# Two cross-attention layers on one core: layer 1's token-wise exponentials turned and laid over the keys, in place of a second set of scores

## The chip, the cores and the metric

The kernel runs on one core of a Trainium2 chip. The metric is the device time of one execution in microseconds (us). The kernel before was timed three times: 987.32 us median, 983.13 to 987.98. A separate execution was recorded by the hardware profiler; all views below are of that one.

The engines are named as the profile names them: PE (TensorE's matrix multiplications), PEld (its loads of the stationary operand), DVE (VectorE), ACT (ScalarE), POOL (GpSimd), SP (SyncE, which issues nearly all transfers). All data are float32. The profile shows each float32 matmul as two records.

## What is computed

Two cross-attention layers, one after the other, over the same 128 context tokens. The batch is 2, the sequence 2048, the width 512, and there are 16 heads. Layer 0 has heads of 64 and a mask; layer 1 has heads of 32, no mask and no biases in its projections. Both end with a residual and a LayerNorm.

```python
def _L1_xattn_ref(query, key, value, Wq, Wk, Wv, Wo, bo, ln_gamma, ln_beta):
    q = _split_heads(query @ Wq.T)                       # (b, 16, 2048, 32)
    k = _split_heads(key @ Wk.T)                         # (b, 16, 128, 32)
    v = _split_heads(value @ Wv.T)
    logits = scaling * jnp.einsum('bhqd,bhkd->bhqk', q, k)
    attn = jax.nn.softmax(logits, axis=-1)
    ctx = jnp.einsum('bhqk,bhkd->bhqd', attn, v)
    ctx = ctx.transpose(0, 2, 1, 3).reshape(query.shape[0], q.shape[2], H)
    projected = ctx @ Wo.T + bo
    resid = query + projected
    ...                                                  # LayerNorm over the width
x = _L0_xattn_ref(x, ctx_1024, ctx_1024, mask, ...)
x = _L1_xattn_ref(x, ctx_1024, ctx_1024, ...)
```

## The kernel before

The 4096 tokens are cut into 8 tiles t of 512. Layer 0's queries, scores, exponentials and values come first, for all tiles (some 373 us). Then a software pipeline runs in rounds: in round t, layer 1's attention of tile t, the output projection and LayerNorm of layer 0 and the query projection of layer 1 for tile n = t + 1, fetches for tile f = t + 2, and the output projection of layer 1 for tile l = t - 1. The order in each round is a list written by hand in `steps(t)`: each entry is a function's letter, its tile and its part. All five engines execute their own instructions in exactly that order; a wait in one engine's stream holds everything behind it on that engine, SP's transfers included. There are five such lists: t = -1, t = 0, the general one, the round before the last tile (n == NB - 1), and the last tile's.

Layer 1's attention works on a tile t and a group g of four heads (r = 0..3), so 4 groups per tile, 28 (tile, group) pairs without the last tile. The steps are:

- `maxima` (X), L866. For each of the four blocks i of 128 tokens and each head r, the scores with tokens on the partitions: the queries are the stationary operand, the keys stream (L873). Two PSUM tiles of two banks each hold them. DVE takes each token's maximum over the 128 keys into `tops` (L879 for heads 2 and 3, L893 for heads 0 and 1). ACT takes the exponentials of heads 2 and 3, eight instructions with the negative maximum as bias (L889). DVE subtracts the maxima of heads 0 and 1 (L894), and ACT takes one exponential over them (L897). The exponentials e serve only for their sums.
- `sums1` (U), L900: DVE sums e over the keys (L903).
- `shares1` (G), L909: reciprocals of the sums, into `tops` beside the maxima.
- `turn_maxima` (M), L913: PE turns `tops`, DVE copies it out (L918), and SP writes the rows to DRAM (L924) and reads them back spread over all partitions: the maxima over the 128 key partitions, 1 MB per group, into `p1` (L927), and the reciprocals over the 32 rows of each head, `r1` (L936).
- `scores1` (S), L941: the scores a second time, now with keys on the partitions (L948). DVE subtracts them and the maxima in `p1` (L967). In the last tile the maxima are subtracted by a matmul with `sel` (L955) and ACT takes the exponential straight from PSUM (L965).
- `exponentials1` (P1), L970: ACT, one exponential over 128 x 2048 (L972).
- `attend1` (V), L974: the values times the exponentials (L996), then DVE multiplies by the reciprocals into `ctx` (`scale1`, L1009).

`project1` (E, L1026) then projects `ctx`, `rest1` (Y, L1033) adds the residual, `moments1` (I), `norm1` (O) and `store` (W) finish the tile. Of layer 0 the rounds hold `load_residual` (F), `fetch_r` (A), `fetch_u` (L), `normalise` (N, POOL, L182), `residual` (R, POOL, L191), `project0` (Pr, L671), `rest0` (J, L678), `moments0` (K0), `norm0` (Z). The queries of layer 1 come from `turn_whole` (TW), `sums_of_turned` (TS) and seven block products `product1` and `add1` (PQ, AQ, L822), or from `turn` and `queries1` (T, Q) in the first two tiles.

PSUM is split into two score tiles with one buffer each (used by X, S and TW), two banks `mm` and two banks `av`.

Of the kernel before, what the change touches and what calls it, by code (L numbers as in the profile page):

```python
# [24 lines left out]
def two_cross_attentions(  # L25
# [81 lines left out]
    sel = const.tile([P, NG, K], F32, tag="sel", name="sel")  # L107
    for g in range(NG):
        for r in range(4):
            rows = slice(32 * r, 32 * (r + 1))  # L110
            nc.vector.tensor_scalar(
                sel[rows, g, :], ident[rows, 32 * r + g : 32 * r + g + 1].to_broadcast([32, K]),
                -1.0, None, ALU.mult,
            )
# [33 lines left out]
    rows_dram = [dram.tile([2 * NG, 4, TB], F32, tag=f"rows_{t}", name=f"rows_{t}") for t in range(NB)]  # L148
# [660 lines left out]
    def product1(t, n):  # L809
# [17 lines left out]
        if n == 1:  # L827
            q1s[t] = two.tile([P, NG, TB], F32, tag="q1", name=f"q1_{t}")
            for m in range(2):
                nc.scalar.activation(  # L830
                    q1s[t][:, m, LO], ps[:, m, :], AF.Identity, bias=bq1[:, 2 + m : 3 + m]
                )
# [21 lines left out]
    def queries1(t, g, half):  # L854
        if g == 0 and half == 0:
            q1s[t] = two.tile([P, NG, TB], F32, tag="q1", name=f"q1_{t}")
# [8 lines left out]

    def maxima(t, g):  # L866
# [3 lines left out]
        for i in range(NQ):  # L870
            for r in range(4):
                rows = slice(32 * r, 32 * (r + 1))
                nc.tensor.matmul(  # L873
                    ps[r // 2][:, r % 2, i, :], q1s[t][rows, g, i * P : (i + 1) * P],
                    k1[rows, g, b * K : (b + 1) * K], start=True, stop=True,
                )
        to = tops.rearrange("p i (r n) -> p r i n", n=32)[:, :, :, g : g + 1]
        to = to.rearrange("p r i o -> p r (i o)")
        nc.vector.tensor_reduce(to[:, 2:], ps[1], AX.X, ALU.max)  # L879
        if t == NB - 1:  # L880
            nc.vector.tensor_reduce(to[:, :2], ps[0], AX.X, ALU.max)
            return

        e = fours.tile([P, 4, NQ, K], F32, tag="p1", name=f"e_{t}_{g}")
        less = three.tile([P, 2, NQ], F32, tag="less", name=f"less_{t}_{g}")
        nc.vector.tensor_scalar_mul(less, to[:, 2:, :], -scaling)  # L886
        for r in range(2, 4):
            for i in range(NQ):
                nc.scalar.activation(  # L889
                    e[:, r, i, :], ps[1][:, r - 2, i, :], AF.Exp, bias=less[:, r - 2, i : i + 1],  # L890
                    scale=scaling,
                )
        nc.vector.tensor_reduce(to[:, :2], ps[0], AX.X, ALU.max)  # L893
        nc.vector.tensor_tensor(  # L894
            e[:, :2], ps[0], to[:, :2, :].unsqueeze(3).to_broadcast([P, 2, NQ, K]), ALU.subtract
        )
        nc.scalar.activation(e[:, :2], e[:, :2], AF.Exp, scale=scaling)  # L897
        open_x[t, g] = e

    def sums1(t, g):  # L900

        to = sums.rearrange("p i r n -> p r i n")[:, :, :, g : g + 1]
        nc.vector.tensor_reduce(  # L903
            to.rearrange("p r i o -> p r (i o)"), open_x.pop((t, g)), AX.X, ALU.add
        )

    tTs, probs1, open_x = {}, {}, {}

    def shares1(t):  # L909
        share = tops.rearrange("p i (r n) -> p i r n", n=32)[:, :, :, NG : 2 * NG]  # L910
        nc.vector.reciprocal(share, sums)

    def turn_maxima(t):  # L913
# [4 lines left out]
        nc.vector.tensor_copy(tT, tr)  # L918
# [4 lines left out]
        for r in range(4):  # L923
            nc.sync.dma_start(rows_dram[t][:, r, :], tT[32 * r : 32 * r + 2 * NG, :])  # L924
        for g in range(NG):
            p1 = fours.tile([P, 2, 2, TB], F32, tag="p1", name=f"p1_{t}_{g}").rearrange("p a b q -> p (a b) q")
            nc.sync.dma_start(p1, rows_dram[t][g].unsqueeze(0).to_broadcast([P, 4, TB]))  # L927
            probs1[t, g] = p1
            if g == NG - 2:
                fetch_r1(t, 0)  # L930
        for g in range(1, NG):
            fetch_r1(t, g)

    def fetch_r1(t, g):
        r = three.tile([P, TB], F32, tag="r1", bufs=4, name=f"r1_{t}_{g}")
        nc.sync.dma_start(r, rows_dram[t][NG + g].unsqueeze(1).to_broadcast([4, 32, TB]))  # L936
        dens1[t, g] = r
# [3 lines left out]
    def scores1(t, g):  # L941

        b, _ = where(t)
        last = t == NB - 1
        ps = sc_tiles(f"s1_{t}_{g}", [2, TB])
        for r in range(4):
# [3 lines left out]
                start=True, stop=not last,  # L950
# [277 lines left out]
```

## Time and profile before

| what | value |
|---|---|
| time of the runs, median (lowest to highest) | 987.32 us (983.13 to 987.98) |
| profiled execution, first to last instruction | 977.3 us; granted PE clock 0.997 |
| layer 0's attention (20 to 373 us) | PE busy 352.2 of 353.0 us, DVE 267.5 |
| start of the rounds (373 to 434) | PE busy 60.4 of 61.0 |
| a second steady round (738.82 to 808.70, 69.88 us) | PE busy 69.88, DVE 59.41, ACT 29.91, POOL 40.20, DMA share 0.45 |
| last tile (878 to 960) | PE busy 80.0 of 82.0 |
| after it (960 to 977.3) | PE busy 7.8 of 17.3 |

The profiled execution's record runs from its first to its last instruction; of its own time outside of that there is no record, and the median of the runs lies 10.0 us above its span. Busy time is the union of an engine's instructions in a window. Matmuls are pipelined and one record of 512 columns spans about 0.6 us while the next one starts 0.44 us after it, so durations of single records add up to more than the time they take; the distance from start to start is the better measure. The idle time of an engine that is not the bound costs nothing.

### The profile page before, as it was taken

Reading aid. Unit: us, or ns where it says so; the run is one execution under the profiler, and the core shown is the slowest. Engines: PE = TensorE matmul, PEld = TensorE weight load, DVE = VectorE, ACT = ScalarE, POOL = GpSimd, SP = SyncE. Lnnn points to the kernel's source line nnn. Section 1 sums busy time; section 2 is a strip of 40 time slices with the busy share of each in tenths; the row PEclk is TensorE's granted clock in tenths of the full one; section 3 lists DMA queues with packets and bytes.
Section 4 is the critical chain, followed back from the end, with each engine's and each line's share of the span. In section 5 each row is a group of like instructions: output and inputs, shape, how many; then the busy total and the mean of one; then the engine's idle time right before and its main releaser. Section 6 shows DMA issues by size and latency. Waiting matters only on the chain.

```text
span 977.3 us, 12755 instructions
## 1 busy us (share of the span) xinstructions
PE 958.0 (98%) x4628; PEld 448.4 (46%) x4628; DVE 731.8 (75%) x1093; ACT 414.9 (42%) x637; POOL 483.3 (49%) x403
## 2 busy tenths in 40 slices
PE   8999999999999999999999999999999999999996
PEld 4444333333333334474544644645545545545442
DVE  2577777878878872249469869879789689698867
ACT  1145345545534644044534434434344444344351
POOL 1044454543453546685453934925835736546153
PEclk9999999999999999999999999999999999999998
DMA  9314265225223436534632542632723724403311
GB/s 337 126 49 141 55 175 155 56 57 182 60 79 86 120 104 201 181 128 157 243 128 87 188 160 87 238 110 89 263 82 119 251 90 155 167 1 151 111 44 43
DMA packets 51325, 128.46 MB, mean 131 GB/s; under 512 B 9440, under 2 KB 13280, under 8 KB 47680
## 3 DMA queue, kind: packets, MB, share of 16 engines
q1 hardware_dynamic: 49536, 125.03, 38.5%
q0 software_dynamic: 1152, 2.10, 0.9%
q8 instruction: 36, 0.59, 0.3%
q10 hardware_dynamic: 576, 0.53, 0.2%
q14 instruction: 25, 0.20, 0.1%
HBM read 101.46 MB, written 26.18 MB: 131 GB/s over the span
## 4 chain that ended last, share of the span: by engine, by line
PE 76%; DVE 4%; POOL 2%; issue 1%; ACT 0%; POOLq 0%; DVEq 0%; ACTq 0%
PE pso L671 22%; PE ps L347 12%; PE pso L1026 10%; PE psq L822 8%; PE psu L491 5%; PE st L396 4%; PE s L948 3%; PE mx L873 3%; PE u L996 3%; PE psq L860 1%; PE tr L727 1%; PE den L470 1%; PE den L484 1%; DVE sums L903 1%; PE psk L591 1%
## 5 line engine op out<-in xcount | busy, mean ns | idle before, releaser
L435 POOL TENSOR_TENSOR sm<-sm,mask 128x1024 f32<-128x1024 f32 x64 | 150.4, 2372 | 202.4 <-ACT sm L434 191.4
L671 PE MATMUL pso<-wo,uT 128*128 128x512 f32 x512 | 229.2, 599 | 0.2 <-POOL uT L182 0.2
L671 PEld LDWEIGHTS pso<-wo,uT 128*128 128x128 f32 x512 | 94.5, 190 | 117.2 <-issue 109.1
L658 POOL TENSOR_TENSOR rstd<-rstd,mhalf 128x1 f32<-128x1 f32 x64 | 35.2, 550 | 213.8 <-DVE shift L662 213.7
L434 ACT ACTIVATE sm<-sm,ncs 128x1024 f32<-128x1024 f32 x64 | 70.0, 1141 | 107.6 <-DVE ncs L431 107.5
L1026 PE MATMUL pso<-wq,ctx 128*128 128x512 f32 x256 | 115.5, 600 | 0.0
L889 ACT ACTIVATE e<-mx,less 128x128 f32<-128x128 f32 x224 | 60.9, 383 | 83.6 <-DVE less L886 83.6
L972 ACT ACTIVATE p<-p 128x2048 f32<-128x2048 f32 x28 | 53.5, 1911 | 97.2 <-DVE p L967 79.5
L409 DVE CUSTOM_DVE_ANT_1 sm<-st,mask 128x1024 f32<-128x1024 f32 x64 | 75.6, 1217 | 20.9 <-DMA mask<-in_maskT_dram 13.5
L967 DVE TENSOR_TENSOR p<-s,p 128x1024 f32<-128x1024 f32 x56 | 65.8, 1217 | 29.2 <-PE s L948 28.6
L347 PE MATMUL ps<-xt,wq 128*128 128x512 f32 x180 | 83.4, 599 | 0.0
L359 DVE TENSOR_TENSOR q<-ps,q 128x512 f32<-128x512 f32 x75 | 51.9, 692 | 39.5 <-PE ps L347 35.3
L182 POOL TENSOR_TENSOR uT<-uT,r 128x1024 f32<-128x1024 f32 x32 | 75.3, 2362 | 3.7 <-issue 1.7
L1026 PEld LDWEIGHTS pso<-wq,ctx 128*128 128x128 f32 x256 | 46.5, 190 | 57.4 <-issue 48.6
L462 DVE TENSOR_TENSOR fold<-fold,sm 64x2048 f32<-64x2048 f32 x22 | 64.5, 2930 | 2.6 <-ACT fold L456 1.9
L903 DVE TENSOR_REDUCE sums<-e 128x16 f32<-128x2048 f32 x28 | 63.8, 2278 | 1.1 <-ACT e L897 1.1
L396 PE MATMUL st<-q,k 64*128 64x512 f32 x256 | 63.6, 615 | 0.0
L491 PE MATMUL psu<-sm,v 128*32 128x512 f32 x512 | 62.1, 598 | 0.8 <-ACT dens L441 0.7
L347 PE MATMUL ps<-t,s 128*128 128x512 f32 x120 | 56.4, 592 | 0.0
L347 PEld LDWEIGHTS ps<-xt,wq 128*128 128x128 f32 x180 | 33.2, 190 | 46.5 <-issue 46.4
L686 ACT ACTIVATE z<-z,shift,rstd 128x512 f32<-128x512 f32 x32 | 26.0, 814 | 66.9 <-POOL shift L663 66.9
L688 POOL TENSOR_TENSOR y<-z,g 128x512 f32<-128x512 f32 x32 | 40.6, 1269 | 23.1 <-ACT z L686 23.1
(154 smaller groups left out, 1511.0 us busy)
## 6 DMA issues: line engine op xcount, KB each, us to landing
p<-rows SPq DMA_DIRECT2D x28, 1024.0 KB
u<-u SPq DMA_DIRECT2D x32, 512.0 KB
uT<-u SPq DMA_DIRECT2D x32, 512.0 KB
xt<-in_xT_dram SPq DMA_DIRECT2D x16, 512.0 KB
z<-in_x_dram SPq DMA_DIRECT2D x32, 256.0 KB
r<-r SPq DMA_DIRECT2D x32, 256.0 KB
out_dram<-y SPq DMA_DIRECT2D x32, 256.0 KB
r<-rows SPq DMA_DIRECT2D x28, 256.0 KB
```

The source lines that it names most:

```text
L182: nc.gpsimd.tensor_tensor(u, u, r.unsqueeze(1).to_broadcast([P, 2, TB]), ALU.mult)
L347: nc.tensor.matmul(ps, w[:, c, :], x[c] if isinstance(x, tuple) else x[:, c, :], start=(c == 0), stop=(c == 1),)
L396: nc.tensor.matmul(st[n][:, j, :], k0[rows, 2 * g + n, b * K : (b + 1) * K], q[rows, :], start=True, stop=True,)
L409: nc.vector.tensor_tensor_reduce(out=sm, in0=st[n], in1=masks[t].unsqueeze(1).to_broadcast([P, 2, TB]), scale=1.0, scalar=-3.4028234e38, o ...
L434: nc.scalar.activation(s, s, AF.Exp, bias=ncs[:, i + n : i + n + 1])
L435: nc.gpsimd.tensor_tensor(s, s, masks[t].unsqueeze(1).to_broadcast([P, 2, TB]), ALU.mult)
L491: nc.tensor.matmul(ps[32 * j : 32 * (j + 1), :], v0[:, b, d : d + 32], p[j], start=True, stop=True,)
L671: nc.tensor.matmul(ps, uTs[t, n // 2][:, n % 2, i * P : (i + 1) * P], wo0s[n // 2][:, n % 2, :], start=(n == 0), stop=(n == NE - 1),)
L822: nc.tensor.matmul(ps[:, m, :], w[:, c, m * P : (m + 1) * P], y[:, c, :], start=(c == 0), stop=(c == 1),)
L903: nc.vector.tensor_reduce(to.rearrange("p r i o -> p r (i o)"), open_x.pop((t, g)), AX.X, ALU.add)
L967: nc.vector.tensor_tensor(p1[:, at], ps[n], p1[:, at], ALU.subtract)
L1026: nc.tensor.matmul(ps, ctxs[t][g][:, i * P : (i + 1) * P], wo1s[:, g, :], start=(g == 0), stop=(g == NG - 1),)
```

## The change

For tiles 0 to 6 the second scores go. The exponentials that `maxima` computes anyway, with tokens on the partitions, are laid out so that they can be turned:

- The four token blocks of `maxima` take every fourth token (`by_fours`): block i holds the tokens 4m + i. So the stationary operand steps by four elements.
- e gets its own tiles (two buffers), ordered as key block, head and token block, key within the block. ACT's eight exponentials also give the sums of their rows (`accum_out`); the maxima go to a small tile `top`, no longer to `tops`.
- `sums1` sums the remaining two heads, then DVE turns e in place in 32x32 blocks (L911 of the new kernel), and SP lays the 4 x 4 blocks over the key partitions with 16 transfers from SBUF to SBUF into `p1` (L915).
- `scores1` stays for the last tile only; its maxima are subtracted through a broadcast column of a negative identity, `minus`, in place of `sel`. `exponentials1` is gone. The broadcast of the maxima through DRAM is gone; that of the reciprocals stays.
- `attend1` reads `p1` in four pieces per head, and `scale1` writes every fourth token of `ctx`, which puts the tokens back in order.
- The queries `q1` have one buffer in place of two. The descriptor scratch of POOL's transfers is set to 2048 bytes.
- All lists of `steps` are written anew; the values of a tile now stand in the next tile's round (in the same round for t = 6).

```diff
     def maxima(t, g):
...
-                    ps[r // 2][:, r % 2, i, :], q1s[t][rows, g, i * P : (i + 1) * P],
+                    ps[r // 2][:, r % 2, i, :], by_fours(q1s[t][rows, g, :])[:, i],
...
+        e = two.tile([P, 4, 4 * NQ, 32], F32, tag="e", name=f"e_{t}_{g}")
+        nc.vector.tensor_reduce(top[:, 1], ps[1], AX.X, ALU.max)
+        nc.vector.tensor_scalar_mul(less, top[:, 1], -scaling)
         for r in range(2, 4):
             for i in range(NQ):
                 nc.scalar.activation(
-                    e[:, r, i, :], ps[1][:, r - 2, i, :], AF.Exp, bias=less[:, r - 2, i : i + 1],
-                    scale=scaling,
+                    e[:, :, r * NQ + i, :], ps[1][:, r - 2, i, :].rearrange("p (k q) -> p k q", q=32),
+                    AF.Exp, bias=less[:, r - 2, i : i + 1], scale=scaling,
+                    accum_out=sums[:, r, i, g : g + 1],
                 )
...
     def sums1(t, g):
 
-        to = sums.rearrange("p i r n -> p r i n")[:, :, :, g : g + 1]
+        e = open_x.pop((t, g))
         nc.vector.tensor_reduce(
-            to.rearrange("p r i o -> p r (i o)"), open_x.pop((t, g)), AX.X, ALU.add
+            sums[:, :2, :, g : g + 1].rearrange("p r i o -> p (r i o)"),
+            e[:, :, : 2 * NQ, :].rearrange("p k m q -> p m k q"), AX.XY, ALU.add,
         )
+        flat = e.rearrange("p k m q -> p (k m q)")
+        nc.vector.transpose(flat, flat)
+        p1 = fours.tile([P, 4, 4, P], F32, tag="p1", name=f"p1_{t}_{g}")
+        for k in range(4):
+            for a in range(4):
+                nc.sync.dma_start(
+                    p1[32 * k : 32 * (k + 1), a].rearrange("p r q -> p (r q)"),
+                    e[32 * a : 32 * (a + 1), k].rearrange("p m q -> p (m q)"),
+                )
+        probs1[t, g] = p1
...
-            p1 = fours.tile([P, 2, 2, TB], F32, tag="p1", name=f"p1_{t}_{g}").rearrange("p a b q -> p (a b) q")
-            nc.sync.dma_start(p1, rows_dram[t][g].unsqueeze(0).to_broadcast([P, 4, TB]))
...
     def scores1(t, g):
...
-                nc.vector.tensor_tensor(p1[:, at], ps[n], p1[:, at], ALU.subtract)
...
-    def exponentials1(t, g):
-        p1 = probs1[t, g]
-        nc.scalar.activation(p1, p1, AF.Exp, scale=scaling)
...
     def scale1(t, g):
-        nc.vector.tensor_tensor(ctxs[t][g], open_u.pop((t, g)), dens1.pop((t, g)), ALU.mult)
+        u, r = (v.rearrange("p (a i q) -> p a i q", a=4, q=32) for v in (open_u.pop((t, g)), dens1.pop((t, g))))
+        nc.vector.tensor_tensor(ctxs[t][g].rearrange("p (a q i) -> p a i q", a=4, i=NQ), u, r, ALU.mult)
...
+        return [
+            (F, f, 0), (R, n, 3), (X, t, 0), (J, n, 0), (A, f, 0), (F, f, 1), (A, f, 1), (V, l, 0), (F, f, 2),
+            (Pr, n, 1, 0), (A, f, 2), (K0, n, 0), (Pr, n, 1, 1), (U, t, 0), (X, t, 1), (Z, n, 0), (A, f, 3),
+            (J, n, 1), (V, l, 1), (K0, n, 1), (Pr, n, 2, 0), (U, t, 1), (Pr, n, 2, 1),
+            *([(R, n, 2)] if t > 1 else []), (X, t, 2), (J, n, 2), (V, l, 2), (K0, n, 2), (Z, n, 1),
+            (Pr, n, 3, 0), (Pr, n, 3, 1), (U, t, 2), (J, n, 3), (L, f, 0), (V, l, 3), (L, f, 1), (X, t, 3),
+            (K0, n, 3), (L, f, 2), (Z, n, 2), (L, f, 3), (F, f, 3), (E, l, 0), (Y, l, 0), (E, l, 1),
+            (Z, n, 3), (U, t, 3), (N, f, 0), (G, t), (N, f, 1), (E, l, 2), (Y, l, 1), (I, l, 1), (I, l, 0),
+            (Y, l, 2), (TW, n), (I, l, 2), (E, l, 3), (TS, n, 0), (N, f, 3), (TS, n, 1), (O, l, 0), (O, l, 1),
+            (N, f, 2), (Y, l, 3), (R, f, 0), (I, l, 3), (M, t), (PQ, n, 2), (PQ, n, 1), (PQ, n, 6), (O, l, 3),
+            (PQ, n, 7), (AQ, n, 6), (PQ, n, 5), (AQ, n, 7), (R, f, 1), (PQ, n, 4), (AQ, n, 2), (PQ, n, 3),
+            (O, l, 2), (AQ, n, 5), (AQ, n, 4), (W, l, 0), (AQ, n, 3), (W, l, 1), (W, l, 2), (Pr, f, 0, 0),
+            (Pr, f, 0, 1), (W, l, 3),
+        ]
...
-    nc = bacc.Bacc("TRN2", target_bir_lowering=False, num_devices=1)
+    nc = bacc.Bacc("TRN2", target_bir_lowering=False, num_devices=1, dynamic_dma_scratch_size=2048)
```

## The prediction, written before the changed kernel was run

> **What bounds the kernel now.** I read the page's busy times first, then the busy time of each engine stage by stage, then one steady round (one 512-token tile) in order of time.
>
> ```profile
> span 977.3 us, 12755 instructions
> PE 958.0 (98%) x4628; PEld 448.4 (46%) x4628; DVE 731.8 (75%) x1093; ACT 414.9 (42%) x637; POOL 483.3 (49%) x403
> ...
> 434.00:505.00 71.00, 68.13 (x389) 35.56 (x386) 46.38 (x58) 31.73 (x68) 38.67 (x35) 1.00 0.56 193
> ...
> 599.05:668.94 69.89, 69.89 (x365) 36.08 (x365) 59.41 (x92) 29.91 (x55) 40.18 (x40) 1.00 0.45 153
> 668.94:738.82 69.88, 69.88 (x366) 36.09 (x365) 59.41 (x92) 29.91 (x55) 40.21 (x40) 1.00 0.44 152
> ```
>
> The columns of the last rows are window, length, busy PE, PEld, DVE, ACT, POOL, then granted clock (1.00). In a steady round PE is busy for the whole 69.88 us. The kernel is as long as its PE work, so only PE work that goes, or PE waits that come, move the time. The second engine is DVE, at 59.4 us of 69.9, and it is not evenly spread:
>
> ```profile
> 597.88 1.17 PE L873 MATMUL mx<-k,q 32*128 32x128 f32 x32
> 598.98 10.73 PE L1026 MATMUL pso<-wq,ctx 128*128 128x512 f32 x24
> ...
> 618.71 1.14 PE L948 MATMUL s<-q,k 32*128 32x512 f32 x8
> 619.78 1.99 PE L822 MATMUL psq<-ts,ws 128*128 128x256 f32 x8
> ...
> 630.22 1.07 PE L996 MATMUL u<-p,v 128*32 128x512 f32 x8
> 631.22 1.99 PE L822 MATMUL psq<-yT,ws 128*128 128x256 f32 x8
> ```
>
> Start to start, maxima of a head group take 1.10 us of PE, second scores 1.07, values 1.00. A full step of layer 0's projection (L671, 16 records) runs 590.81 to 597.88, 7.07.
>
> ```profile
> L967 DVE TENSOR_TENSOR p<-s,p 128x1024 f32<-128x1024 f32 x56 | 65.8, 1217 | 29.2 <-PE s L948 28.6
> L903 DVE TENSOR_REDUCE sums<-e 128x16 f32<-128x2048 f32 x28 | 63.8, 2278 | 1.1 <-ACT e L897 1.1
> L996 PEld LDWEIGHTS u<-p,v 128*32 128x32 f32 x256 | 5.7, 108 | 24.2 <-ACT p L972 10.6 <-issue 9.4 <-ACT y L1041 3.8
> L873 PEld LDWEIGHTS mx<-k,q 32*128 32x128 f32 x1024 | 31.5, 186 | 25.2 <-issue 24.4 <-DVE p L967 0.8
> ```
>
> **Removed.** PE: four matmuls (eight records) for each of 28 (tile, group) pairs, 28 x 1.07 = 30.0 us, 4.28 per round; all of it is on the bound. DVE: 56 subtractions of 1.217 = 68.2 us. ACT: 28 exponentials (L972) of 1.911 = 53.5 us. The 28 row broadcasts of 1 MB go too. The last tile keeps its second scores, so its 4 pairs gain nothing; its `sel` weights become a broadcast of `minus`, 16 matmuls with as many columns, price nothing within 0.1 us each.
>
> **Added on ACT.** 224 exponentials get a sum; the one accumulator row that exists (L785) has a read of 0.19 us behind each ACTIVATE. Eight per group: 1.5 us, so the eight exponentials take 2.18 + 1.5 = 3.7 us. ACT has 40 us free per round, and the next user of those PSUM banks comes 9 us later; without that cover it would be 1.5 us for each of 28 pairs, 43 us.
>
> **Added on DVE.** The sum covers half the elements: 2.278 becomes about 1.14, saving 1.14. Then one 32x32 block transpose of 128x2048 in place, not in this trace. Nearest rows: the reduce over the same 2048 elements, 2.278; lower end, half of it, 1.14; upper end, twice, 4.56 (one pass to fill, one to drain). I take 2.28, equal shape and count. The division after the values (L1009, 0.69) writes every fourth element: between 0.69 and, doubled, 1.37; I take 0.69. DVE per round: 59.4 - 9.7 - 4.6 + 9.1 = 54.2, still less than PE's.
>
> But the work is not where it was. The first three quarters of a round are maxima of a group, layer 0's projection of a block, and DVE's share of both. Before: DVE 1.22 + 0.45 + 1.21 + 1.22 (maxima, L879 to L894), 0.68 (L678), 1.07 (statistics), 2.28 (sums) = 8.13, against PE 1.10 + 7.07 = 8.17: level. After, the values of the tile before are put into each quarter: PE 9.17; DVE 8.13 + 1.14 + 0.69 = 9.96. DVE falls behind by 0.79 per quarter. DVE's clock from the round's start: 1.2 + 3 x 9.96 = 31.1; the fourth block's residual and division 1.37, last maxima 4.1, statistics 1.07, first output residual (L1033) 0.68: 38.3. PE: 3 x 9.17 + 1.00 + 1.10 + two output projections of 3.54 = 36.7, and the third needs the bank that this residual empties. PE waits 1.6. Later DVE has less to do (no subtractions) and catches up.
>
> **Moved.** Second use of the queries is gone, so one buffer suffices; only the maxima read it. Values of tile t move into round t+1, their wait on exponentials (L996 above: 10.6 us of weight loads) goes; what they wait for now are transfers a round older.
>
> **Added on SP.** Sixteen transfers of 64 KB per pair, 448 in all, for 28 removed. An issue of a small transfer has a row:
>
> ```profile
> 612.04 1.30 SPq L924 DMA_DIRECT2D rows<-tT  x4
> ```
>
> 0.32 each, 5.2 us per pair, 20.8 per round. Range: 0.29 (the shortest group, L924's median) to 1.37 (uT, 5.47 us for 4, 512 KB each). I take 0.32. In the changed program's order each transfer also waits for the eighth before it in the queue; SP's waits show 2.3 us at most for a rows transfer to land, less than eight issues of 0.32. Behind the transposes' wait stand, in the queue, uT fetches (issued by my clock near 37, wanted by POOL at 42), stores, loads of the next residuals. Cover: tile `e` of a group is written again two groups later. Sums of group 0 end at 11.2; group 2's subtraction starts near 24; 12.8 us for 5.2 + 2.3. Were it late, that subtraction would hold all of DVE behind it, and the exponentials all of ACT, and PE would wait at the next maxima. [...]
>
> POOL's descriptor scratch shrinks; it serves the 8 mask loads (L234, 4.7 us in all). Between nothing and twice that, all in layer 0 where PE is busy 352.2 of 353 us; I take nothing.
>
> **Added on the weight loads.** The maxima's stationary operand is every fourth token, a step of 16 bytes; all weight loads in the trace are dense. 128 columns take 186 ns (L873), 32 take 108 (L996): 78 ns for 96 columns, 104 for 128. Lower end: nothing. Upper end: column time doubles and all shows: 32 records on four row strips, eight per strip, 8 x 0.104 = 0.83 us per group, 32 groups = 26.6 us. I take nothing: the load group's busy 0.98 of 1.10 us is overlapped, and the rows give no reason for a penalty. [...]
>
> **Sum.** A steady round: 69.88 - 4.28 + 1.6 = 67.2, a gain of 2.7; five of them, 13.5. Round t=0 (434 to 505): DVE has no division there and lags 1.1 per quarter less than its free time; 4.28 less about 0.8 for the fourth block, 3.5. Round t=6: 2.7. Last tile: nothing. Together 19.7. 977.3 - 19.7 = 957.6 for the span. The runs' median 987.32 lies 10.0 above the span; I keep that: 967.6, so **968**. Own range: without any wait 30.0 + 1.3 (waits in 434 to 505 on exponentials) gives 956; some quarters' division at 1.37 (lag +0.68 per quarter, 2 us per round, 14 in all) gives 981.
>
> **Rivals.** (a) Strided weight loads cost their upper end. A quarter of PE is then 10.0, level with DVE, and the 1.6 us wait vanishes: 69.88 - 4.28 + 3.3 = 68.9, gain 1.0 in five rounds and in t=6, 2.3 in t=0, minus 3.3 for the last tile's maxima: 5 in all, **982**. For: maxima are the group with the most weight columns per streamed column, so a slow load shows there first. Against: the loads are busy 31.5 us of the maxima's 37.6, which leaves room for part of it only if they overlap.
> (b) DVE becomes the bound of the first half of a round (the slower side). Place: the transposes behind the sums. The round is back at 69.88 when the wait grows by 2.7, that is 0.9 per quarter: from 3.2 us per transpose. At 4.56: three quarters each 2.28 later, 6.8 more, round 74.0, 4.1 over seven rounds = 29: **1016**. For: DVE was level already. Against: 2048 elements of float32 cost 2.28 in the reduce.
> (c) SP's queue becomes the bound. From (12.8 - 2.3) / 16 = 0.65 us per transfer, `e` is late. At 1.0 us a group takes 16 us against quarters of 9.96; groups 2 and 3 wait 5.5 and 6 us, 11 per round, less the 2.7: 8 over seven rounds: **1045**. For: transfers of 512 KB cost 1.37. Against: 0.32 for 16 KB.
>
> **How the numbers follow.** Within 0.5% (4.9 us) counts as no change: 982.4 to 992.3; a measurement of this kernel can't tell less, its three runs spread by 4.8. Forecast 0.47, wholly faster. (a) 0.25, half each side of 982.4: 0.12 faster, 0.13 same. (b) 0.17 and (c) 0.11, slower. Faster 0.59, same 0.13, slower 0.28. The range takes 950 (a few us below no wait at all, for covered waits that the trace hides) to 1005, which takes in (a) and the milder half of (b): some 0.15 lie above, 0.05 below.
>
> **What would show it.** Right: 28 fewer score groups, PE busy near 928; steady rounds near 67 with an idle of 1 to 2 us before the third output projection, released by DVE; transpose rows near 2.28. (a): maxima near 1.9 us start to start. (b): transposes above 3.2, maxima waiting for DVE. (c): transfers above 0.65 us, and subtractions or exponentials of the maxima released by a transfer. Wrong altogether if rounds wait where I saw cover: on uT at layer 0's projection or on p at the values.

## The result, and the profile after

The changed kernel takes 1044.99 us (median of 4 runs, 1043.72 to 1045.28) against 985.94 us for the kernel before on the same chip: a ratio of 1.0604 (95% interval 1.0581 to 1.0627). It is slower by 59 us, where 968 us and a range of 950 to 1005 had been predicted. The page of the profiled execution, and its steady rounds (window, length, busy PE, PEld, DVE, ACT, POOL, granted clock, DMA share, GB/s):

```profile
span 1042.8 us, 13088 instructions
...
PE 973.6 (93%) x4404; PEld 481.6 (46%) x4404; DVE 702.7 (67%) x1050; ACT 377.5 (36%) x833; POOL 484.1 (46%) x403
...
611.17:682.96 71.79, 68.94 (x334) 38.93 (x333) 54.83 (x87) 24.40 (x82) 38.33 (x40) 1.00 0.50 145
682.96:757.86 74.90, 70.97 (x334) 39.96 (x333) 55.60 (x87) 24.39 (x82) 41.75 (x42) 0.98 0.49 143
757.86:832.04 74.18, 70.92 (x333) 40.03 (x332) 54.65 (x87) 24.40 (x82) 40.04 (x41) 0.98 0.48 142
```

Two things are to be seen. The 224 PE records (8 x 28) of the second scores are gone, but PE is busy for 973.6 us and not for 928. And PE, busy for 98% of the span before, is now busy for 93%: it waits. A round takes 71.8 to 74.9 us where it took 69.9. The groups of instructions that answer to those shown before (line, engine, operation, count; busy us, mean ns of one; idle before):

```profile
L870 PEld LDWEIGHTS mx<-k,q 32*128 32x128 f32 x1024 | 62.7, 322 | 25.9 <-issue 24.4
L870 PE MATMUL mx<-k,q 32*128 32x128 f32 x1024 | 68.8, 405 | 0.7 <-DVE tops L878 0.7
L911 DVE STREAM_TRANSPOSE e<-e 128x2048 f32<-128x2048 f32 x28 | 64.7, 2312 | 1.0
L906 DVE TENSOR_REDUCE sums<-e 128x8 f32<-128x1024 f32 x28 | 34.0, 1215 | 6.8 <-ACT e L900 6.6
L1006 DVE TENSOR_TENSOR ctx<-u,r 128x512 f32<-128x512 f32 x28 | 31.0, 1108 | 6.7 <-DMA r<-rows 4.6 <-PE u L992 2.0
```

A weight load of the maxima went from 186 to 322 ns, and their matmuls' busy time from 37.6 (the prediction's (a)) to 68.8 us: this alone eats the 30.0 us that were removed. It leaves some 14 of the 45 us by which PE's busy time misses 928; where they come from is seen with the flat transfer below. DVE's new work has about the sizes that were forecast: 2.31 us for a transpose, 1.215 for the half sum; the division is 1.108, between the two ends given (0.69 was taken). Now a steady round in order of time, PE first, then two lines of SP's own queue, one from before this round and one from within it:

```profile
682.96 2.15 PE L870 MATMUL mx<-k,q 32*128 32x128 f32 x32
685.03 1.06 PE L992 MATMUL u<-p,v 128*32 128x512 f32 x8
...
742.09 3.68 PE L816 MATMUL psq<-yT,wq 128*128 128x256 f32 x8 [3.74 <-ACT q L824]
```

```profile
659.00 12.91 SPq L915 DMA_DIRECT2D p<-e  x16
...
696.29 11.11 SPq L915 DMA_DIRECT2D p<-e  x16
```

Start to start the maxima of a group take 2.07 us here (1.10 before). The sixteen transfers of one pair occupy SP for 11 to 13 us, 0.7 to 0.8 us each, while the DMA engines are only half busy (DMA share 0.49 above): it looks as if the issuing were full, not the bytes, which is tested below. A quarter of a round is some 10 us, and SP's queue then runs from 696.29 to 745.18 us without a gap of more than 0.2 us. How that reaches PE is clearest in round t = 0, where SP's queue reads:

```profile
476.21 12.25 SPq L915 DMA_DIRECT2D p<-e  x16
488.57 0.52 SPq L181 DMA_DIRECT2D z<-in_x_dram  x1
...
490.95 14.33 SPq L915 DMA_DIRECT2D p<-e  x16
505.32 0.58 SPq L171 DMA_DIRECT2D r<-r  x1
506.00 1.36 SPq L166 DMA_DIRECT2D uT<-u  x3
507.47 15.43 SPq L915 DMA_DIRECT2D p<-e  x16
522.99 0.53 SPq L166 DMA_DIRECT2D uT<-u  x1
523.57 0.57 SPq L171 DMA_DIRECT2D r<-r  x1
```

and PE in the same stretch:

```profile
515.20 1.99 PE L665 MATMUL pso<-wo,uT 128*128 128x512 f32 x4 [3.71 <-POOL uT L176]
518.12 1.98 PE L665 MATMUL pso<-wo,uT 128*128 128x512 f32 x4 [0.93 <-POOL uT L176]
532.36 3.78 PE L665 MATMUL pso<-wo,uT 128*128 128x512 f32 x4 [8.74 <-POOL uT L176]
```

The fourth fetch of `uT` and of `r` for layer 0's projection stands behind sixteen transfers that have nothing to do with it. They go out at 523, land some 6 us later, POOL's normalisation takes 2.35 us, and PE, which had nothing else in its order, starts at 532.36. In steady rounds the path is longer, but seems to have the same start. SP issues the fetches of `uT` from 729.69 us on, POOL's multiplications of `uT` start at 733.54 after 3.60 us of idle time, ACT's whitening then waits 9.44 us for POOL, ACT's copies of the queries come behind it, and PE waits 3.74 us at `psq`. Five rounds have such a wait, of 2.9 to 3.7 us. That POOL waits for the fetches there is inferred; with the flat transfer below POOL waits for `uT` once in the whole run (13.0 us), its idle time before these multiplications is 16.8 us in all in place of 49.1, and PE's wait for ACT at this `psq` (16.2 us in all) is gone. In the waits of ACT, the exponentials of the maxima stand behind the transfers, since `e` is not free:

```profile
ACT e L887 <- DMA p<-e: 81.9, 12, 10.9
```

(us in total, times, longest.) And the shares by line of the chain that ended last, where PE had 76% in all before and has 26% now:

```profile
SPq L915 11%; PE pso L665 8%; DMA r<-r 8%; PE pso L1023 4%; DMA uT<-u 4%; PE mx L870 3%; PE psq L854 3%; PE psq L816 2%; POOL uT L176 2%; POOL y L1041 1%; PE u L992 1%; PE ps L341 1%; POOL y L1044 1%; DMA out_dram<-y 1%; DMA p<-e 1%
```

So there are two suspects, the step of 16 bytes in the weight loads and the number of issues on SP, and a third that can't be excluded from the traces: the new order of the lists.

### The profile page after: what moved, and what is told of

Same layout as the page of the kernel before. It is cut to its first block, busy times and chain, and to the rows that moved or that the text cites. A ratio compares the mean times of both kernels' runs of the same rounds, so it can differ in the third digit from the quotient of the medians.

```text
span 1042.8 us, 13088 instructions
## 1 busy us (share of the span) xinstructions
PE 973.6 (93%) x4404; PEld 481.6 (46%) x4404; DVE 702.7 (67%) x1050; ACT 377.5 (36%) x833; POOL 484.1 (46%) x403
## 4 chain that ended last, share of the span: by engine, by line
PE 26%; DMA 17%; SPq 13%; POOL 6%; DVE 3%; issue 3%; ACT 2%; POOLq 0%; ACTq 0%; DVEq 0%
SPq L915 11%; PE pso L665 8%; DMA r<-r 8%; PE pso L1023 4%; DMA uT<-u 4%; PE mx L870 3%; PE psq L854 3%; PE psq L816 2%; POOL uT L176 2%; POOL y L1041 1%; PE u L992 1%; PE ps L341 1%; POOL y L1044 1%; DMA out_dram<-y 1%; DMA p<-e 1%
## 5 line engine op out<-in xcount | busy, mean ns | idle before, releaser
L665 PE MATMUL pso<-wo,uT 128*128 128x512 f32 x512 | 230.1, 602 | 15.3 <-POOL uT L176 15.3
L887 ACT ACTIVATE e<-mx,less 128x128 f32<-128x128 f32 x224 | 78.8, 378 | 197.1 <-DMA p<-e 81.9
L176 POOL TENSOR_TENSOR uT<-uT,r 128x1024 f32<-128x1024 f32 x32 | 75.1, 2354 | 49.1 <-DMA uT<-u 18.1
L883 DVE TENSOR_REDUCE top<-mx 128x8 f32<-128x1024 f32 x28 | 34.0, 1214 | 76.1 <-PE mx L870 76.1
L1038 ACT ACTIVATE y<-y,shift,rstd 128x512 f32<-128x512 f32 x30 | 23.3, 811 | 144.2 <-POOL shift L657 144.2
L870 PEld LDWEIGHTS mx<-k,q 32*128 32x128 f32 x1024 | 62.7, 322 | 25.9 <-issue 24.4
L870 PE MATMUL mx<-k,q 32*128 32x128 f32 x1024 | 68.8, 405 | 0.7 <-DVE tops L878 0.7
L911 DVE STREAM_TRANSPOSE e<-e 128x2048 f32<-128x2048 f32 x28 | 64.7, 2312 | 1.0
```

The lines of the kernel that those rows point to most:

```text
L176: nc.gpsimd.tensor_tensor(u, u, r.unsqueeze(1).to_broadcast([P, 2, TB]), ALU.mult)
L665: nc.tensor.matmul(ps, uTs[t, n // 2][:, n % 2, i * P : (i + 1) * P], wo0s[n // 2][:, n % 2, :], start=(n == 0), stop=(n == NE - 1),)
L870: nc.tensor.matmul(ps[r // 2][:, r % 2, i, :], by_fours(q1s[t][rows, g, :])[:, i], k1[rows, g, b * K : (b + 1) * K], start=True, stop=True,)
L887: nc.scalar.activation(e[:, :, r * NQ + i, :], ps[1][:, r - 2, i, :].rearrange("p (k q) -> p k q", q=32), AF.Exp, bias=less[:, r - 2, i : ...
L911: nc.vector.transpose(flat, flat)
```

## The experiments

All times are medians; each ratio is to the kernel before, timed beside it, with its 95% interval. The kernel before took 985.94 us beside the changed kernel and 982.2 to 983.3 beside the others, so a difference between the changed kernel and another holds to some 3 us; the ratios are given where that matters. "Dense blocks" means the changed kernel with blocks of 128 neighbouring tokens in place of every fourth.

### The weight loads by fours, put into the kernel before

```diff
-  q1s[t][rows, g, i * P : (i + 1) * P],
+  q1s[t][rows, g, :].rearrange("p (m i) -> p i m", i=NQ)[:, i],
```

with the turned maxima put back in order where they are copied.

> The kernel before with one part of the change: the maxima's stationary operand takes every fourth token (the copy of the turned rows puts the tokens back in order). Theory 1, the strided weight loads cost PE by themselves: in the changed kernel the maxima step from start to start is 2.08 us against 1.10, 32 groups x 0.98 = 31 us; the kernel before is PE-bound, so about 985.9 + 31 = 1017 us, maxima at 2.08. Theory 2, the loads are slow only because the new transfers load the memory at the same time: maxima stay at 1.10 and the time at 986 to 988.

Measured: 1010.12 us, ratio 1.0273 (1.0258 to 1.0288). PE stays the bound, busy for 990.6 of 1008.0 us. Its groups for the maxima:

```profile
L873 PEld LDWEIGHTS mx<-k,q 32*128 32x128 f32 x1024 | 62.9, 322 | 24.7 <-issue 23.2
...
L873 PE MATMUL mx<-k,q 32*128 32x128 f32 x1024 | 69.0, 405 | 0.7 <-DVE tops L881 0.7
```

They match the changed kernel's 62.7 and 68.8. Nothing else of the change is in this kernel, so the loads by fours cost 27 us by themselves.

### Dense blocks in the changed kernel

```diff
-  by_fours(q1s[t][rows, g, :])[:, i],
+  q1s[t][rows, g, i * P : (i + 1) * P],
...
-  ctxs[t][g].rearrange("p (a q i) -> p a i q", a=4, i=NQ)
+  ctxs[t][g].rearrange("p (i a q) -> p a i q", a=4, i=NQ)
```

> The changed kernel with dense weight loads: blocks of 128 neighbouring tokens again, the order put back in the division and in the last tile's copy. Theory 1 (strided loads): maxima back at 1.10, 31 us of PE work less, 1045 - 31 = 1014 us if the waits stay what they are (PE busy about 942). Theory 2 (the waits came because the rounds were tuned to faster transfers and are the larger part): PE was the slower party for some of the time, so shorter maxima turn partly into more waits, 1020 to 1035. Division on VectorE (writes every fourth element, 1.11 us now) back to 0.69.

Measured: 1034.49 us, ratio 1.0523 (1.0495 to 1.0552): 10 us less than the changed kernel (8 by the ratios), not 27. With the loads dense, PE waits longer instead (it is busy for 92% of the span). So in the changed kernel most of the slower loads lies inside time in which PE would have waited anyway, and the larger cost is elsewhere.

### The lists of before, without their second scores

On top of dense blocks, all lists of `steps` are those of the kernel before, less the entries S and P1; the values stand in their own round again.

> As n_blocks, but with the order of the kernel before in every round, minus the second scores and their exponentials; the values stay in their own tile's round. Theory 3, the new lists are what puts GpSimd's and ScalarE's work behind late transfers: waits at the start (17 us until the first maxima, 17 more in the round of tile 0) vanish and the time is 955 to 970. Theory 2, the 448 transfers themselves make the fetches late whatever the order: waits stay, 985 to 1015.

Measured: 1028.43 us, ratio 1.0457 (1.0431 to 1.0483). The old order is nearly as far from the kernel before as the new one (4.6% against 5.2%), so the order of the lists is not the main cause; with the flat transfer below, the new lists reach 957 us. In its trace the forty-eight transfers of three pairs stand in one row:

```profile
685.07 33.46 SPq L915 DMA_DIRECT2D p<-e  x48
```

33.46 / 48 = 0.70 us each.

### POOL's descriptor scratch alone

```diff
-  nc = bacc.Bacc("TRN2", target_bir_lowering=False, num_devices=1)
+  nc = bacc.Bacc("TRN2", target_bir_lowering=False, num_devices=1, dynamic_dma_scratch_size=2048)
```

> The kernel before with the descriptor scratch at 2048 bytes and nothing else. In the changed kernel layer 0's attention, whose code is the same, ends 4.4 us later. If the scratch does it: about 990 us. If it is the spread of single executions: 986 within 2.

Measured: 982.48 us, ratio 0.9989 (0.9980 to 0.9999): nothing, as the prediction had it.

### Sixteen transfers per pair, put into the kernel before

```diff
+        for k in range(4):
+            for a in range(4):
+                nc.sync.dma_start(
+                    extra[32 * k : 32 * (k + 1), a],
+                    sel[32 * a : 32 * (a + 1)].rearrange("p g k -> p (g k)"),
+                )
```

They are 64 KB each and stand behind each group's sums. No one reads `extra`; the computation is that of the kernel before. The descriptor scratch is at 2048 bytes here too.

> The disputed cost by itself: the kernel before, with sixteen more transfers of 64 KB from SBUF to SBUF behind each of 28 sums, from a constant into a tile that nobody reads (descriptor scratch at 2048 bytes to make room). Theory A, SyncE's issue is the price: 0.59 us of issue, 0.70 from one to the next, 45 us of SyncE per round beside some 25 that are there; stores, fetches and row broadcasts queue behind, and the time goes to 1005 to 1035. Theory B, it was the dependence of the tiles (e, p1) on the transfers that made the waits, not the queue: nothing here depends on them, so 983 to 988.

Measured: 1096.96 us, ratio 1.1153 (1.1124 to 1.1181). The transfers alone, with no strided load and no new list, cost 115 us, more than expected. In PE's waits (total, times, longest):

```profile
PE s L954 <- DVE p L973: 95.7, 6, 22.4
```

DVE's subtraction waits for the broadcast `p` of the maxima (119.8 us in all), which in the kernel before stands in SP's queue in the same round, behind the new transfers. That broadcast is gone in the changed kernel, so this one price can't be carried over to it; what it shows is that transfers of this kind, with nothing else changed, make what stands behind them in the queue late.

### One flat transfer per pair in place of sixteen

Dense blocks and the changed lists.

```diff
-        for k in range(4):
-            for a in range(4):
-                nc.sync.dma_start(p1[32 * k : 32 * (k + 1), a]..., e[32 * a : 32 * (a + 1), k]...)
+        nc.sync.dma_start(p1.rearrange("p a r q -> p (a r q)"), flat)
```

It moves the same 1 MB per pair from `e` to `p1`, but leaves out the laying of the blocks over all keys.

> n_blocks (dense weight loads, new lists) with one flat transfer of 1 MB from e to p1 in place of the sixteen of 64 KB: the same bytes and the same dependences; it leaves out the laying of key blocks over the partitions. Theory A (the number of issues on SyncE): the waits go, PE busy near 945, time 957 to 972. Theory B (the bytes, or the dependence on any transfer): waits stay, 1010 to 1034.

Measured: 957.12 us, ratio 0.9742 (0.9723 to 0.9761), 77 us faster than with sixteen transfers and 25.1 faster than the kernel before (982.25). A page line, a steady round, and from PE's waits the one that the prediction had named:

```profile
PE 928.2 (97%) x4404; PEld 443.9 (46%) x4404; DVE 692.3 (72%) x1050; ACT 377.0 (39%) x833; POOL 482.4 (51%) x403
```

```profile
635.09:700.68 65.59, 65.21 (x333) 34.95 (x332) 53.92 (x87) 24.35 (x82) 39.95 (x41) 1.00 0.46 162
```

```profile
PE pso L1018 <- DVE y L1025: 2.5, 5, 1.1
```

This is what the prediction had forecast for the changed kernel: PE busy for 928 us, a wait for DVE before the third output projection, five times. The round is 65.6 us, 69.88 less 4.28, since that wait is 0.5 us on average (2.5 over 5) and not 1.6. The bytes moved in a round are as many as with sixteen transfers (161 to 162 GB/s here against 142 to 145 over longer rounds), so it was not the bytes. One flat transfer is also wider, 128 partitions for 32. That narrow transfers are not the price by themselves is seen below: with five issues per pair, four of them into 32 partitions, the steady rounds take 65.6 us as well.

### The same flat transfer with the loads by fours

The changed kernel whole, with the flat transfer in place of the sixteen; the laying over all keys is left out.

> The changed kernel whole (weight loads of the maxima by fours, its lists), but with one flat transfer of 1 MB per pair in place of sixteen; left out is the laying over all keys, so the tiles of p1 keep the transposed blocks where they are. Theory: the two costs, SP's sixteen issues and the strided weight loads, add where each is free to show; with the queue free, PE is the bound, and the loads by fours cost their whole 0.98 us per group: 957 of the dense kernel with the flat transfer plus 27 to 31, so 984 to 988, with maxima 2.08 us start to start and PE busy some 955 to 960. Rival: in the lists of the changed kernel DVE sets the pace of the first three quarters of a round (the 1.6 us wait and what is spread), so part of the slower maxima lies beside DVE's work and the cost is only the 10 us that were seen with the sixteen transfers in place: 965 to 970.

Measured: 982.58 us, ratio 1.0001 (0.9991 to 1.0012). With the queue free, the loads by fours show their cost, 25.5 us (982.6 - 957.1), with PE busy for 98% of the span. Its page line, and the first maxima of two rounds that follow each other:

```profile
PE 958.0 (98%) x4404; PEld 476.4 (49%) x4404; DVE 700.9 (71%) x1050; ACT 377.9 (39%) x833; POOL 482.5 (49%) x403
```

```profile
575.80 2.15 PE L870 MATMUL mx<-k,q 32*128 32x128 f32 x32
...
644.48 2.15 PE L870 MATMUL mx<-k,q 32*128 32x128 f32 x32
```

A round is 68.68 us. The changed kernel's 1045 is then 957.1, plus 25.5 for the loads, plus 62.4 for the sixteen issues (59 by the ratios). The two costs hide each other in part: taken in the other order they are 77.4 for the issues and 10.5 for the loads (77 and 8 by the ratios).

Nor are the 62 us all waiting. PE executes the same instructions here and in the changed kernel, in 958.0 us of busy time here and 973.6 there. Of the 62.3 us between the two spans (1042.8 less 980.5), 46.7 are idle time of PE and 15.6 are slower matmuls, at a mean granted clock of 0.975 there and 0.993 here. The slow ones stand near the long waits: in the lines of round t = 0 above, the four records behind the wait of 8.74 us take 3.78 us, those behind the waits of 3.71 and 0.93 us take 1.99 and 1.98, and the granted clock from 520 to 540 us is 0.74.

Whether issuing some of the sixteen transfers from another engine's queue would do (ACT is busy for 24.4 us of a round) was not tried.

### Laying the key blocks through DRAM

These kernels lay the blocks over all keys with fewer issues: `e` is written to DRAM in four transfers of 256 KB, and `p1` is read back in one of 1 MB. Dense blocks; with the changed lists, and with the old ones.

```diff
+        for a in range(4):
+            nc.sync.dma_start(lay_dram[t, g][:, :, a, :]..., e[32 * a : 32 * (a + 1)]...)
+        nc.sync.dma_start(p1..., lay_dram[t, g]...)
```

> n_blocks with the key blocks laid by way of DRAM: four transfers of 256 KB out (one per group of 32 partitions of e), one of 1 MB in, so 5 issues for 16, twice the bytes. Theory A: 5 x 0.7 = 3.5 us of SyncE per pair for 11; time 960 to 980. Theory B, bytes: DMA share rises by a quarter, time 1010 or more.

> The same way by DRAM with the order of the kernel before (n_oldlists). Values come later in the round than in the new lists, VectorE has no division in the first half. Theory A: 955 to 975. Were the new lists needed for the gain: slower than n_bounce by 5 us or more.

Measured: 1006.85 us (1.0249, 1.0214 to 1.0283) and 991.98 us (1.0092, 1.0070 to 1.0113). Both are faster than with sixteen issues and slower than the flat one. SP's waits in the first of them (total, times, longest):

```profile
SPq L923 <- DMA lay<-e: 166.3, 52, 8.4
```

Five issues are cheap (in a steady round four writes hold SP for 3.00 us from 675.39 us on, and their read takes 0.34), but the read stands in SP's queue until its own writes have landed (it goes out at 682.53), and everything behind it stands too. A wait in the queue holds it as an issue does. What that costs depends on the order: under the old lists SP waits nearly as long for these writes (138.0 us, 46 times), and the kernel is 15 us faster than under the new ones.

The next two read a pair in one quarter of a round later, behind the next pair's write, with one write of 1 MB and four reads of 256 KB:

```diff
+        nc.sync.dma_start(lay_dram[t, g]..., flat)
+        if g:
+            read_in(t, g - 1)
```

The last pair's read stands behind the turning of the maxima.

> Dense blocks and the changed kernel's lists; the key blocks are laid through DRAM, one write of 1 MB per pair, flat, and four reads of 256 KB each, issued one quarter of a round later (behind the next pair's write, the last pair's behind the turning of the maxima), so that no read stands in SP's queue waiting for its own write to land. All is computed as in the reference. Theory (what SP's queue is held for is the price, bytes are not): five issues per pair, some 3 us instead of 11, and no wait in the queue: the flat kernel's 957 plus little, 957 to 970, faster than the kernel before. Rival: the bytes are the price (1 MB written and 1 MB read per pair, twice what the sixteen transfers move, on top of the row broadcasts): then it stays near the 1007 of the kernel that read in at once, 990 to 1010.

> The same laying through DRAM with late reads, under the lists of the kernel before without the second scores, with the values of a tile in its own round. Theory (SP's hold of the queue is the price): the reads of the last pair and the row broadcasts must land in the same round before the values are used, so some wait stays, 965 to 985; more than under the changed kernel's lists, which give a round for it. Rival: the changed lists bring nothing, and the old ones are better as they were with the read at once (992 against 1007): below the other kernel of this call by some 10 us.

Measured: 983.88 us (1.0024, 1.0013 to 1.0035) with the changed lists, 1004.30 us (1.0228, 1.0209 to 1.0247) with the old ones, which need the values in the same round. The old order, ahead by 15 us with the read at once, is behind by 20 with the late read. In the first kernel SP waits 40.4 us for the writes in place of 166.3, and the steady rounds are 65.6 us, as with the flat transfer; place and shape of the transfers have changed together. What it loses lies in round t = 0 and in the one before the last tile:

```profile
PE pso L670 <- POOL uT L181: 12.3, 3, 6.9
PE psq L821 <- DVE q L851: 5.0, 1, 5.0
```

The next kernel moves all reads of t = 0 behind the row broadcasts, and in every round the last pair's too.

> The kernel with late reads, and two moves of transfers in SP's queue: in round t=0 no read-in stands between the fetches of uT (all four pairs are read in behind the row broadcasts), and in every round the last pair's read-in stands behind the row broadcasts instead of ahead of them. Dense blocks, the changed lists; all is computed as in the reference. Theory: with late reads the steady rounds already take 65.6 us, and what is lost against the flat kernel lies in two places, 12.2 us of waits for uT at layer 0's projection in round t=0, where the transfers fill 1.0 of the DMA engines' time for some 40 us, and 5.0 us for layer 1's queries before the last tile, where the values' division waits for row broadcasts behind eight reads; with both gone (and the lower granted clock behind the long waits) 984 becomes 957 to 966, faster than the kernel before. Rival: the DMA engines themselves are full there, and the wait only moves to the values of round t=1: 972 to 984.

Measured: 991.06 us (1.0094, 1.0077 to 1.0111), a miss; the rival was right that the wait moves, and its time (972 to 984) was passed as well. The waits for `uT` are gone, and PE waits for `p` at the values in their place. PE's waits, then SP's queue behind the broadcasts:

```profile
PE u L1002 <- DMA p<-lay: 19.4, 2, 12.5
```

```profile
497.11 24.83 SPq L924 DMA_DIRECT2D p<-lay  x16
```

Sixteen reads of 256 KB, each into 32 partitions, take 24.83 us, 1.55 each: 4.19 MB / 24.83 us = 169 GB/s. Whether the width of these reads or their place in the queue is the price is what the last pair of kernels asks. Both spread the reads over the gaps of the queue: one of tile 0's behind the third sums, one behind the rows, one behind the broadcasts, one in round 1, and the last pair's of every round between rows and broadcasts. The second has the narrow transfers on the writing side, and reads 1 MB over 128 partitions at once (places and bytes are the same):

```diff
-        nc.sync.dma_start(lay_dram[t, g]..., flat)
+        for a in range(4):
+            nc.sync.dma_start(lay_dram[t, g][:, :, a, :]..., e[32 * a : 32 * (a + 1)]...)
...
-        for k in range(4):
-            nc.sync.dma_start(p1[32 * k : 32 * (k + 1)]..., lay_dram[t, g]...[k])
+        nc.sync.dma_start(p1..., lay_dram[t, g]...)
```

> Late reads through DRAM as before, one write of 1 MB and four reads of 256 KB per pair; the reads are spread over the gaps of SP's queue: in every round the last pair's stands between the writes of the rows and their broadcasts (SP waits there some 5 us for the rows to land), and tile 0's pairs are read in one at a time (behind the third sums, behind the rows, behind the broadcasts, and behind the first sums of round t=1). All is computed as in the reference. Theory (the place in the queue is the price): the waits for uT, for p and for the last tile's queries go, 957 to 968, faster than the kernel before. Rival (the transfers are the price): tile 0's values or uT still come late by 5 to 12 us, 974 to 990.

> The same places and bytes, but four writes of 256 KB from 32 partitions each and one read of 1 MB over 128 partitions. All is computed as in the reference. If the width of a read decides (256 KB into 32 partitions took 1.55 us each when sixteen stood in a row, 169 GB/s, an estimate from that row), p lands earlier and this is faster than the other kernel of this call by 3 to 10 us; if the price is the place in the queue alone, the two are within 5 us, this one perhaps slower because tile e is held by four narrow writes instead of one wide one (exponentials of the maxima waiting for lay).

Measured: 980.45 us (0.9981, 0.9968 to 0.9994) and 967.97 us (0.9856, 0.9824 to 0.9887). The second is faster than both kernels, by 1.4% than the one before, and does all of the work. SP's queue at the same place (behind the rows of t = 0) in the one and in the other:

```profile
493.02 1.29 SPq L951 DMA_DIRECT2D rows<-tT  x4
494.35 9.08 SPq L928 DMA_DIRECT2D p<-lay  x4
504.17 2.18 SPq L955 DMA_DIRECT2D r<-rows  x4
```

```profile
492.65 2.67 SPq L953 DMA_DIRECT2D rows<-tT  x4
495.71 0.35 SPq L931 DMA_DIRECT2D p<-lay  x1
502.16 2.39 SPq L957 DMA_DIRECT2D r<-rows  x4
```

Four narrow reads hold SP for 9.08 us, one wide read for 0.35. At this place little comes of it, since the broadcasts behind start at 504.17 and 502.16 us, when the rows have landed. More than half of the gain lies in round t = 1, where PE waits at the values of tile 0's last pair, in the one and in the other:

```profile
545.05 1.94 PE L1007 MATMUL u<-p,v 128*32 128x512 f32 x8 [9.96 <-DVE shift L661]
```

```profile
536.06 1.06 PE L1009 MATMUL u<-p,v 128*32 128x512 f32 x8 [2.73 <-DMA p<-lay]
```

In the first PE waits for DVE, and DVE's subtraction of the maxima had waited 10.90 us for `e`, until a write of `e` to DRAM had landed; ACT's exponentials waited for the same write:

```profile
ACT e L892 <- DMA lay<-e: 22.5, 2, 16.7
```

In the second such a wait is not among ACT's nine largest, which end at 22.2 us in all. So the gain may come in part through writes that land earlier; whether the wide read or the narrow writes brought that is not separated. The four writes cost SP mostly some 2.8 us per pair, up to 5. Why the narrow reads hold the queue so much longer than the narrow writes was not tried; that these reads start while the writes of other pairs are still landing would be one explanation, and is only argued.

## Why the prediction was wrong

**Removed: right.** PE lost 30.0 us of matmuls; where nothing else stood against it (one flat transfer, dense blocks), PE was busy for 928.2 us, the 928 that was named as the sign, and the time fell by 25.1 us, between the 19.7 of the sum and the 31.3 of no waits. That it fell to 957.1, close to the forecast's lower end of 956, is in part luck of the base: the prediction added 10.0 us to the span for 987.32, but the kernel before took 982.25 beside the flat one, and the profiled executions of the experiments lie only 1.8 to 2.3 us above their spans.

**Added on SP: the step that failed first, by size.** The sum took 0.32 us per transfer from a row of four 16 KB writes, and so 5.2 us per pair, which the cover of 12.8 us seemed to hold. The transfers of 64 KB from partitions to partitions took 0.59 us by themselves (507/589/1802 ns, minimum, median, maximum) and 0.70 to 0.8 one after the other in steady rounds: 11 to 13 us per pair, and 10 to 15 in round t = 0. The range given, 0.29 to 1.37, held this, and rival (c) set the turning point at 0.65 us; the measured value lies just beyond it. The row chosen was the nearest in name (an issue of a small transfer) but not in kind: 512 KB fetches at 1.37 us and small writes at 0.32 lay on both sides of it, and the sum took the lower one. Price: 62 us on the kernel with loads by fours, 77 without them. One of the prediction's own signs of being wrong altogether came with it, PE's waits on `uT` at layer 0's projection. By stages, from the start of one tile's maxima to the next one's:

| stage | before | after | one flat transfer, dense |
|---|---|---|---|
| start to tile 0 | 433.8 | 451.1 | 446.5 |
| round t = 0 | 68.4 | 84.9 | 58.1 |
| round t = 1 | 71.2 | 75.1 | 65.0 |
| rounds t = 2 to 5 | 279.5 | 295.8 | 262.2 |
| round t = 6 | 63.2 | 71.1 | 62.5 |
| last tile | 61.2 | 64.8 | 60.7 |

The first rows must be read together: the new list for t = -1 does some of round 0's work ahead of tile 0's maxima, with the flat transfer as well. Against the last column, rounds t = 0 to 6 of the changed kernel lose 79 us; 3.1 us per steady round of it are the loads (68.7 less 65.6).

**Rival (c)'s time was right, its mechanism only in part.** At 1.0 us per transfer it gave 1045, which happens to be the result at 0.7. It named the late `e`, and ACT did wait 81.9 us for it. But it did not follow what else stands in that queue. The prediction had listed uT fetches "behind the transposes' wait", and then costed only e's reuse. PE's largest waits were for layer 1's queries, by ACT and POOL (16.2 us), and for `uT` (15.3 us). A round that holds SP for 4 x 12 us of transfers leaves some 25 us for all fetches and stores, and these come at the end of the round.

**Added on the weight loads: failed by size.** Taken as nothing, with an upper end of 0.83 us per group, 26.6 in all. Measured: 0.98 (2.08 less 1.10), just above that end, and 25.5 to 27 us in all where PE is the bound. Rival (a) had 982 for this case and 68.9 us for a round; with the queue free it was 982.6 and 68.7. The round is the real agreement: 982 was meant as a gain of 5 us, and against the kernel before beside it (982.22) there was none. A load of 128 columns took 322 ns with a step of 16 bytes against 186 dense. No other step was tried, so what makes the stepped loads slow is not shown. Overlap was the reason to take nothing, and overlap couldn't hold: the loads were already busy for 0.98 of a group's 1.10 us; they became busy for 0.98 us more per group (62.7 less 31.5 over 32), and the group became longer by as much.

**Added on DVE, added on ACT: within the ranges.** Transpose 2.31 (taken 2.28), sum 1.215 (1.14), read of the accumulator 0.217 (0.19); the division took 1.11 where 0.69 was taken (up to 1.37). Rival (b) needs 3.2 us per transpose and falls. The 1.6 us wait before the third output projection is there with the flat transfer, but 0.5 us long on average, 1.1 at most.

**Moved: right as far as the lists go.** Values a round later waited for no transfer in the steady rounds, and under the lists of before the late reads cost 20 us more (1004 against 984). It is not so in every case: with the read at once the old lists were 15 us faster (992 against 1007). The scratch cost nothing.

**The chances.** Rivals (a) and (c) were held as alternatives, with 0.25 and 0.11. They are two costs on two resources, and both came: 25.5 + 62.4 us. No case stood for both together.

## What to carry to other kernels

A queue's price followed the count here, not the bytes (1034.5 us with sixteen transfers of 64 KB per pair, 957.1 with one of 1 MB): multiply the issues by the spacing of transfers of the same kind (here 0.7 us for 64 KB from 32 partitions to 32), compare with the time between two refills (here some 10 us), and then list everything that stands behind them in that queue, not only what they feed. A wait inside a queue held what stood behind it like an issue (166.3 us in all with the read at once); a read that waits for its own write belongs a stage later, in a gap where the queue waits anyway, if the order of the work gives it that stage (1007 to 984 us with the changed lists, but 992 to 1004 with the old ones). And look at how long a group's weight loads are beside the group: here they were busy for 0.98 of 1.10 us, and the slower access to the stationary operand was paid in full.

## What the runs showed that was not expected

- A float32 weight load of 128 columns in 32 rows takes 322 ns with a step of 16 bytes and 186 dense; the 32 records of a group then take 2.08 us in place of 1.10. The same tokens, permuted, gave the whole difference.
- Issues of 64 KB between groups of 32 partitions follow each other at 0.70 us at a DMA share of 0.42; one issue of 1 MB over 128 partitions is 0.51.
- The same 448 issues cost 115 us in the kernel before, 77 in the changed one with dense blocks, and 62 (59 by the ratios) with loads by fours: a queue has no price by itself.
- One read of 1 MB over 128 partitions in place of four of 256 KB into 32, with four writes in place of one, was worth 12.5 us (980.45 to 967.97) with bytes and places unchanged.
- A quarter of what the sixteen issues cost is not idle time: 15.6 of 62.3 us are matmuls that ran slower, at a mean granted clock of 0.975 against 0.993.
